# Selective scans of two hybrid layers beside piecewise side work: pieces that tell how long they hold PSUM, and a shifted order of rows, copies and stores

## The chip, the core and the metric

The kernel runs on one core of a Trainium2 chip. The metric is the device time of one execution in microseconds (us). The program is one launch that takes the whole network from its inputs in HBM to its output in HBM. The core's engines are TensorE (PE; PEld is its weight load), VectorE (DVE), ScalarE (ACT), GpSimd (POOL), and SyncE (SP), whose queue issues the DMA transfers here.

## The reference

`x` has shape (4, 64, 64, 96) in float32: four images of 64 x 64 positions with 96 channels. Layers 0 and 1 each add a gated selective scan of the group-normalized `x`; layers 2 and 3 are token-wise (linear attention and a feed-forward part whose operands are rounded to an 8-bit float format).

```
x = x + scan_layer_0(group_norm(x));  x = x + scan_layer_1(group_norm(x))
t = tokens(x)
for l in (2, 3): t = t + attention_l(ln(t));  t = t + quantized_ffn_l(ln(t))

def scan_layer(x):                                  # 192 inner channels, N = 16 states
    xi, z = split(x @ in_proj_w.T)
    xc = silu(depthwise_conv3x3(xi) + conv_b)
    for k in range(4):                              # four orders (directions) of the 4096 positions
        u = xc in order k
        dts, B, C = split(x_proj_w[k] @ u)
        dt = softplus(dt_w[k] @ dts + dt_b[k])
        h[t] = exp(dt[t] * A) * h[t-1] + dt[t] * u[t] * B[t]       # per channel and state
        y_k[t] = sum over states of h[t] * C[t]  +  D[k] * u[t]
    y = layernorm(y_0 + y_1 + y_2 + y_3, each back in the image's order)
    return (y * silu(z)) @ out_proj_w.T
```

In layer 0 the four directions are rows, columns, and both reversed. In layer 1 they are rows, and windows of 2, 4 and 8 positions.

## The kernel before

**The main loop.** Two images form a pair, and a layer of a pair is a *phase*: phases 0 and 1 are layer 0, phases 2 and 3 layer 1. Each phase has four directions k, each direction four blocks of TB = 1024 time steps. These 64 blocks are run one after the other, and a block is named phase.direction.block, counted from 0. A block has 48 *tiles*: two groups of eight state numbers n, by three thirds j of the channels, by the eight n of the group. A tile's number in its block, 0 to 47, is its *place*. A tile is 128 partitions (64 channels times two states) by 1024 steps; each n stands for two states of one image.

The loop (L1045 to L1095) runs `i` over all 3072 tiles and issues for each `i`, by hand and in this order, work of several tiles. `begin(i + 2)` (L646) makes the scan's first operand: for n in `POOL_N = (1, 4, 7, 10, 13)` a GpSimd product of du with a row of B (L652), otherwise `decays`, the ScalarE Exp (L669). `row(i + 2)` (L657) spreads the row of B over the partitions of a PSUM tile with PE (L662), for the other n. `scan(i)` (L678) is the VectorE scan (L684), followed by a ScalarE copy of the last column, the state (L690). `product(i + 1)` is the VectorE product in PSUM (L676). `weigh(i)` (L692) is the GpSimd product with a row of C (L695). `gather` (L720) folds the states of two tiles on PE into `psY` (L727). After eight tiles `flush(i - 3)` (L732) copies the sum out of `psY` on ScalarE (L739, or L743 after the second group); the second one then issues the store of `ynew` to `yd` in DRAM (L744). `resume` (L706) adds the older sum on PE (L718), and `recall(i + 7)` loads it (`yold`, L704).

**Rows.** `rows_of` (L626) lists, for every tile, the rows of C (`crep`) 7 tiles ahead and those of B (`brep`) 9 tiles ahead; `spread` (L636, L642) issues each as two broadcast DMAs from `bc` in DRAM. They share a ring of 11 buffers.

**The next block.** At place 0, `prepare` (L501) lays out, by place, what the next block needs: loads of the convolution's output (L529, `xraw` L532 for k other than 0), a permuting copy (L538), the projection on PE (L543), the copy `rows` (L549) and its store to `bc` (L555), `cut` (L559) and `take` (L564, L565) for three bf16 parts, `steps` (L569), `biased` (L576), `softplus` (L582), the input product `inputs` on GpSimd (L585), and `twice` (L587, L592), twelve copies by DMA for `deltas` and twelve for `dus`, which put one image's 64 channels on both halves of a tile. With base = 18 for k = 0 and 14 otherwise, the projection begins at place base and the softplus is at base + 15. `prepare` returns the places base - 1 to base + 14 as *kept*: in these no side work runs.

**Side work in pieces.** The convolution of a coming phase (`conv_pieces`, L212), the tail of a finished phase (`tail_pieces`, L313) and the loading of later weights (`mlp_weights`, L167) are generators, chained by `behind` (L997). Each `yield` ends a *piece*, and `advance()` runs the next piece, one at each tile outside the kept places. A piece says at its end `False`, `True` (a PSUM slot of `psM` is still in use) or `MORE` (a convolution tap follows). After `MORE` a second piece runs in the same tile if `late_by` says that the convolution is behind. At the first kept place, `while holds: advance()` runs, in that one tile, as many pieces as it takes to free the slot; at the first place with a task of the next block, pieces are forced until the convolution rows that this block reads are done. This document calls three or more pieces in one tile a *heap*. `psM`, for all side work and the next block, has 2 slots; `psB` has 2, `psY` 1.

A convolution row-pair (`t`) is: its pads, loaded in the piece before (`load` at L260, L273), normalized by ScalarE (L283); then for each j nine taps of two matmuls (L289), the SiLU `xo` (L296), two matmuls for z (L299), the SiLU `zo` (L304) and both stores (L305, L306), the last three in one piece with `xo`. A tail unit of 256 positions is: loads of `yu` and `zu` (L320, L321) and of `xr` at the unit's start, transposes (L360), statistics on ScalarE (L346 and after), the power on GpSimd (L372), normalizing (L380), transposes back (L387), scaling (L392), gates on VectorE (L398), the out-projection with its residual in two pieces, one for each image (L440 and L442, or L426 and L428 where the output is tokens), the copies `xn` on ScalarE and their stores.

On PE, DVE, ACT and POOL the instructions run in the order of the program text as the generators unroll it. SP's order is set by the framework's scheduler, so its DMAs stand in an order of their own. After the loop, `run` (L758) schedules layers 2 and 3 from lists of steps, with what is left of the last phase's tail among them.

Of the kernel before, what the change touches and what calls it, by code (L numbers as in the profile page):

```python
# [15 lines left out]
C = 96  # L16
# [6 lines left out]
T = 512  # L23
# [11 lines left out]
def kernel(ctx: ExitStack, tc: tile.TileContext, ins, out, layers=(0, 1, 2, 3)):  # L35
# [131 lines left out]
    def mlp_weights():  # L167
# [11 lines left out]
        def quantized(q, src, shape):  # L179
            t = wide(shape, "wq")  # L180
            nc.sync.dma_start(t, src)
            yield False
            yield False
            nc.vector.tensor_copy(q, t, saturate=False)
# [22 lines left out]
    MORE = 2  # L207
# [4 lines left out]
    def conv_pieces(w, xin, xc, zg, done):  # L212
# [9 lines left out]
        yield False  # L222
        yield False
        for i in range(2):
            stats = small([C, NT, 6], "gst")
            for t in range(NT):
                if t:
                    yield False
                nc.vector.bn_stats(stats[:, t, :], xbs.pop(0))
                if i * NT + t + 3 < 2 * NT:  # L230
                    xbs.append(part_of(i * NT + t + 3))
            mv = small([C, 2], "gmv")
            nc.vector.bn_aggr(mv, stats)
            yield False
            pm = psM([C, 1])
            nc.tensor.matmul(pm, gmat, mv[:, 0:1], start=True, stop=True)
            yield True
            mean = small([C, 1], "gmean")
            nc.vector.tensor_copy(mean, pm)
            dev = small([C, 1], "gdev")  # L240
            nc.vector.tensor_sub(dev, mv[:, 0:1], mean)
            nc.vector.tensor_mul(dev, dev, dev)
            nc.vector.tensor_add(dev, dev, mv[:, 1:2])
            yield False
            pv = psM([C, 1])
            nc.tensor.matmul(pv, gmat, dev, start=True, stop=True)
            yield True
            t = small([C, 1], "grs")
            nc.vector.tensor_scalar_add(t, pv, 1e-5)
            scale = small([C, 1], f"gscale{i}")  # L250
            nc.gpsimd.tensor_tensor(scale, t, mhalf[0:C, 0:1], ALU.pow)
            yield False
            shift = small([C, 1], f"gshift{i}")
            nc.vector.scalar_tensor_tensor(shift, mean, -1.0, scale, ALU.mult, ALU.mult)
            norms.append((scale, shift))
# [20 lines left out]

        done.append(now[0])
        coming = load(0)
        for t in range(NT):
            pads, coming = coming, None  # L280
            yield False
            for i in range(2):
                nc.scalar.activation(pads[i][1], pads[i][1], AF.Identity, bias=norms[i][1], scale=norms[i][0])  # L283
            yield False
            for j in range(J):
                px = psM([128, T])
                for tap in range(9):
# [6 lines left out]
                    yield MORE if tap < 8 else True  # L294
# [3 lines left out]
                for i in range(2):  # L298
# [3 lines left out]
                    )  # L302
                zo = thin([128, T], "zo")
                nc.scalar.activation(zo, pz, AF.Silu)  # L304
                nc.sync.dma_start(xc[:, j, t * T : (t + 1) * T], xo)  # L305
                nc.sync.dma_start(zg[:, j, t * T : (t + 1) * T], zo)  # L306
                if j == J - 1 and t + 1 < NT:
                    coming = load(t + 1)
                if j == J - 1:
                    done[0] += 1  # L310
                yield False

    def tail_pieces(w, units, y, zg, xin, xout, tokens):  # L313
# [10 lines left out]
        coming = None  # L324
        for t in units:
            tt = slice(t * U, (t + 1) * U)
            if coming is None:
                while t * U >= flushed(y):
                    yield False
                coming = load(t)  # L330
                yield False
                yield False
# [4 lines left out]
            xr = st([C, 2, U], F32, "xr", 1)  # L337
            for i in range(2):
                nc.sync.dma_start(xr[:, i, :], xin[i][:, tt])
# [17 lines left out]
            for q in range(2):  # L357
# [5 lines left out]
                if q:  # L363
                    statistics(0, pts)
                pts = pt
                yield True
            statistics(1, pts)
            yield False
# [5 lines left out]
            yield False  # L374
            yield False
# [25 lines left out]
            yield False  # L401
            pn0 = back(0)
            normalize(1)
            yield True
            scaled(pn0)
            pn1 = back(1)
            yield True
            scaled(pn1)
            yield True
            gate(0, pn0)  # L410
# [3 lines left out]
            yield True  # L414
            gate(1, pn1)
            yield True
            if tokens:
                xo = thin([128, 2, 2, C], "xn")
                pos = []
                for i in range(2):  # L420
# [8 lines left out]
                    yield True  # L429
                for i in range(2):  # L430
                    nc.scalar.copy(xo[:, i], pos[i][:, :, 0:C])
                    nc.sync.dma_start(xout[i][tt].rearrange("(q p) c -> p q c", p=128), xo[:, i])
                ready[0] = t + 1
            else:
                xo = thin([C, 2, U], "xn")
                pos = []
                for i in range(2):
# [5 lines left out]
                    yield True  # L443
                for i in range(2):
                    nc.scalar.copy(xo[:, i, :], pos[i])
                    nc.sync.dma_start(xout[i][:, tt], xo[:, i, :])
            yield False
# [53 lines left out]
    def prepare(ph, k, t):  # L501
# [47 lines left out]
        def rows(s):  # L549
# [4 lines left out]
            nc.scalar.copy(rests[s], pps[s])  # L554
            nc.sync.dma_start(p["bc"][:, halves[s]], rests[s][0 : 4 * N])  # L555
# [45 lines left out]
        for j in range(J):  # L601
# [10 lines left out]
            copies = max(32 + 8 * j, base + 17)  # L612
# [4 lines left out]
        for s in range(2):  # L617
            at(base + 3 + s, rows, s)
            for q in range(3):
# [6 lines left out]
    def rows_of(at, g):  # L626
# [3 lines left out]
        for n in range(g * GN, (g + 1) * GN):  # L630
            for v in (0, 1):
                if v or n in POOL_N:
                    out.append((first + n - g * GN - (7 if v else 9), at, v, n))
# [98 lines left out]
    def flush(i):  # L732
# [11 lines left out]
        nc.sync.dma_start(made[at]["img"](yd[ph][:, j, :]), yb)  # L744
# [270 lines left out]
    made, reps, sums, states, scanned, order = {}, {}, {}, {}, {}, [None]  # L1015
    end = len(tiles)
    now, rest = [0], (L - TB) // 256
    with tc.manual_schedule(engines=MANUAL):
# [9 lines left out]
        aside, holds, todo = None, False, {}  # L1028

        def advance():  # L1030
            nonlocal aside, holds
            holds = next(aside, None) if aside is not None else None
            if holds is None:
                aside = None
# [11 lines left out]
        for i in range(-9, end + 4):  # L1046
# [22 lines left out]
            if 0 <= i < end:  # L1069
# [5 lines left out]
                if plan:  # L1075
# [9 lines left out]
                    if place == kept[0]:  # L1085
                        while holds:
# [3 lines left out]
                if aside is not None and not (plan and place in kept):  # L1090
                    advance()
                    if holds == MORE and late_by(i, blocks[at][0]):
# [119 lines left out]
```

## Time and profile before

| what | value |
|---|---|
| median of three runs | 11,167.48 us (11,153.49 to 11,181.56) |
| profiled execution | 11,149.85 us |
| its span | 11,148.1 us |
| mean granted clock of TensorE | 0.87 |
| busy PE, DVE, ACT, POOL | 80%, 89%, 58%, 92% of the span |
| first scan starts, last scan ends | 134.5 us, 10,545.7 us |
| DMA | 1,604.57 MB, mean 144 GB/s |

A line of the profile's group view gives source line, engine, operation, the tile written and those read with partitions x elements and type, the number of instructions; then busy time and mean ns of one; then the idle time of the engine just before these, and which instruction ended most of it. A line of the wait view says who waited for whom: us in total, times, longest. A timeline line gives the start and the duration in us, engine, line, operation; a bracket at its end holds the idle time just before it and what ended it. "SPq" is the issue of a DMA on SP's queue: its duration there is the time that the issue took, not the transfer. A line of the windows view gives a stretch, its length, and each engine's busy time with the number of instructions, then TensorE's granted clock, the mean busy share of the DMA engines and GB/s.

### The profile page before, as it was taken

What the parts mean: (1) busy time and instruction counts of PE and PEld (TensorE: products, weight loads), DVE (VectorE), ACT (ScalarE), POOL (GpSimd) and SP (SyncE); (2) the same over time, 40 slices, a digit from 0 to 9 for tenths busy, and PEclk for the clock granted to TensorE, in tenths of its full rate; (3) what the DMA queues carried; (4) which work ended last, traced back from release to release, by engine and by line L of the source; (5) the groups of instructions that cost most, each with busy time, mean ns of one, the idle gap of its engine ahead of it and who ended that gap; (6) DMA issues with size and microseconds to landing.
All of it is one profiled execution on the core that took longest, in us unless ns stands there. A gap on an engine that the chain in (4) does not pass through costs nothing. (4 is left out here: it accounts for less than half of the span.)

```text
span 11148.1 us, 101994 instructions
## 1 busy us (share of the span) xinstructions
PE 8910.0 (80%) x30112; PEld 2880.5 (26%) x30112; DVE 9926.4 (89%) x6431; ACT 6423.1 (58%) x10575; POOL 10204.6 (92%) x5102
## 2 busy tenths in 40 slices
PE   7978888777777779887788878887778877778777
PEld 2222222111222212221222222222222322222365
DVE  3898999999999889989999999999999999999846
ACT  3656556554566646665566656665466655555576
POOL 3989999999999889999999999999999999999846
PEclk8989999888888889998888889998888888888877
DMA  5679976897578885798666656665556565556410
GB/s 134 158 141 162 141 160 157 145 134 136 149 171 151 140 151 149 157 159 132 138 169 157 157 146 169 164 159 143 149 157 156 155 149 148 143 137 159 122 33 22
DMA packets 1848188, 1604.57 MB, mean 144 GB/s; under 512 B 1412298, under 2 KB 1482892, under 8 KB 1847628
## 3 DMA queue, kind: packets, MB, share of 16 engines
q1 hardware_dynamic: 1847628, 1598.04, 66.1%
q8 instruction: 237, 3.88, 0.2%
q14 instruction: 323, 2.65, 0.1%
HBM read 1008.37 MB, written 186.65 MB: 107 GB/s over the span
## 5 line engine op out<-in xcount | busy, mean ns | idle before, releaser
L695 POOL TENSOR_TENSOR f<-f,crep 128x1024 f32<-128x1024 f32 x3072 | 7158.9, 2354 | 395.9 <-DVE f L684 296.6
L727 PE MATMUL psY<-f,fold 128*64 128x512 f32 x12288 | 3795.1, 698 | 183.4 <-POOL f L695 182.8
L684 DVE TENSOR_TENSOR_SCAN f<-f,state,psB 128x1024 f32<-128x1024 f32 x1584 | 3717.8, 2347 | 206.2 <-ACT f L669 50.1
L669 ACT ACTIVATE f<-delta,L_a 128x1024 f32<-128x1024 f32 x2112 | 2406.5, 1145 | 903.9 <-PE psY L727 829.8
L676 DVE TENSOR_TENSOR psB<-psB,du 128x1024 f32<-128x1024 f32 x2112 | 2558.9, 1212 | 362.9 <-PE psB L662 322.1
L662 PE MATMUL psB<-spB,sel 96*128 96x512 bf16 x4224 | 1387.8, 414 | 1613.5 <-DVE f L684 1599.0
L652 POOL TENSOR_TENSOR f<-du,brep 128x1024 f32<-128x1024 f32 x960 | 2265.7, 2360 | 127.2 <-PE psY L727 29.4
L684 DVE TENSOR_TENSOR_SCAN f<-psB,state,f 128x1024 f32<-128x1024 f32 x720 | 1676.7, 2329 | 76.8 <-POOL f L652 50.3
L727 PEld LDWEIGHTS psY<-f,fold 128*64 128x64 f32 x12288 | 974.9, 154 | 2525.3 <-issue 1806.8
L690 ACT COPY state<-f 128x1 f32<-128x1 f32 x2304 | 429.7, 188 | 2065.8 <-DVE f L684 2056.7
L669 ACT ACTIVATE psB<-delta,L_a 128x1024 f32<-128x1024 f32 x960 | 1070.2, 1115 | 696.0 <-DVE f L684 636.1
L684 DVE TENSOR_TENSOR_SCAN f<-f,psB 128x1024 f32<-128x1024 f32 x528 | 1208.3, 2288 | 57.6 <-ACT f L669 5.9
L662 PEld LDWEIGHTS <-sel 96*128 96x128 bf16 x4224 | 271.3, 99 | 3320.4 <-DVE f L684 2163.7
L289 PE MATMUL psM<-pad,wf 96*64 96x512 f32 x3456 | 901.4, 623 | 36.0 <-ACT pad L283 28.9
L684 DVE TENSOR_TENSOR_SCAN f<-psB,f 128x1024 f32<-128x1024 f32 x240 | 545.6, 2273 | 102.9 <-ACT psB L669 60.0
L718 PE MATMUL psY<-ysum,ident 128*128 128x512 f32 x768 | 554.5, 862 | 98.3 <-ACT ynew L743 86.7
L585 POOL TENSOR_TENSOR xs<-delta,xs 128x1024 f32<-128x1024 f32 x192 | 452.7, 2358 | 95.0 <-ACT delta L582 95.0
L569 PE MATMUL psM<-proj,dtw 12*128 12x512 f32 x768 | 455.2, 686 | 0.0
L543 PE MATMUL psM<-xs,xp 128*76 128x512 f32 x768 | 414.7, 651 | 5.5 <-DMA xs<-xcd 4.2
L718 PE MATMUL psY<-yold,ident 128*128 128x512 f32 (+2 forms) x960 | 370.6, 526 | 42.2 <-ACT ysum L739 26.7
L289 PEld LDWEIGHTS psM<-pad,wf 96*64 96x64 f32 x3456 | 221.4, 138 | 501.0 <-issue 422.6
L743 ACT COPY ynew<-psY 128x1024 f32<-128x1024 f32 (+2 forms) x312 | 242.4, 818 | 171.5 <-PE psY L727 171.5
(149 smaller groups left out, 6644.6 us busy)
## 6 DMA issues: line engine op xcount, KB each, us to landing
crep<-bc SPq DMA_DIRECT2D x2048, 256.0 KB, 4.8
delta<-delta SPq DMA_DIRECT2D x768, 256.0 KB, 4.8
du<-xs SPq DMA_DIRECT2D x768, 256.0 KB, 6.2
brep<-bc SPq DMA_DIRECT2D x640, 256.0 KB, 4.9
yd<-ynew SPq DMA_DIRECT2D x192, 512.0 KB, 7.8
xraw<-xcd SPq DMA_DIRECT2D x144, 512.0 KB, 8.5
yold<-yd SPq DMA_DIRECT2D x144, 512.0 KB, 8.9
xcd<-xo SPq DMA_DIRECT2D x96, 256.0 KB, 3.0
```

The lines of the kernel that those rows point to most:

```text
L289: nc.tensor.matmul(px[64 * i : 64 * i + 64], w["wf"][:, tap, 64 * j : 64 * j + 64], pads[i][0][:, tap // 3 : tap // 3 + rows, tap % 3 : ta ...
L569: nc.tensor.matmul(pds[-1], order[0][1][64:76, j, :], rests[s][64:76], start=True, stop=True)
L585: nc.gpsimd.tensor_mul(xs[j], deltas[j], xs[j])
L652: nc.gpsimd.tensor_mul(f[:, 1:], made[at]["dus"][j][n % 2], reps[at, 0, n])
L662: nc.tensor.matmul(scanned[i][0][:, ss], sel[:, n, :], made[at]["parts"][:, ss], start=True, stop=True)
L669: nc.scalar.activation(out, made[at]["deltas"][j][n % 2], AF.Exp, scale=W[phases[ph][0]]["a"][:, k, j, n // 2 : n // 2 + 1])
L676: nc.vector.tensor_mul(scanned[i][0], scanned[i][0], made[at]["dus"][j][n % 2])
L684: nc.vector.tensor_tensor_scan(f[:, 1:], a, bu, 0.0 if t == 0 else states[at - 1][:, c : c + 1], ALU.mult, ALU.add)
L690: nc.scalar.copy(states[at][:, c : c + 1], f[:, TB : TB + 1])
L695: nc.gpsimd.tensor_mul(f[:, 0:TB], f[:, 1:], reps[at, 1, n])
L718: nc.tensor.matmul(o, of, v, start=(m % banks == 0), stop=False)
L727: nc.tensor.matmul(py[64 * e : 64 * e + 64, ss], fold, two[e][:, ss], start=False, stop=(n == g * GN + GN - 1),)
```

## The change

Pieces now end with a tuple: `free(ahead)` says that no PSUM slot is held, and that a sequence of `ahead` pieces follows that should fit before the kept places; `held(left, more)` says that a slot is held for `left` more pieces. The loop computes the `room` left before the kept places and runs a piece after a `free` only if `ahead` fits in it; a second piece runs after a tap if the convolution is late or if `left` would otherwise not fit. The convolution and the tail are re-cut: `xo` and the z matmuls are one piece and `zo` the next, z's store and the tail's output stores are issued one or more pieces later, the next pads are loaded at the start of the last j, four tiles instead of two stand between a first load and its use, `xr` is loaded after the first normalizing, and the gates come after the next unit's loads. The store of `bc` comes two tiles after the copy `rows`, rows 5 and 7 tiles ahead instead of 7 and 9, copies at 34 + 8j instead of max(32 + 8j, base + 17), and the store of `ynew` two tiles after `flush`. Line numbers shift by up to 29 in the kernel after.

```diff
-    MORE = 2
+    def free(ahead=0):
+        return 0, ahead, False
+
+    def held(left, more=False):
+        return left, 0, more
...
         xbs = [part_of(n) for n in range(3)]
-        yield False
-        yield False
+        for _ in range(4):
+            yield free()
...
         coming = load(0)
+        yield free()
+        yield free()
         for t in range(NT):
             pads, coming = coming, None
-            yield False
...
-            yield False
+            yield free(6)
             for j in range(J):
+                if outs:
+                    outs.pop()()
+                if j == J - 1 and t + 1 < NT:
+                    coming = load(t + 1)
...
-                    yield MORE if tap < 8 else True
+                    yield held(10 - tap, tap < 8)
...
+                yield held(1)
                 zo = thin([128, T], "zo")
                 nc.scalar.activation(zo, pz, AF.Silu)
                 nc.sync.dma_start(xc[:, j, t * T : (t + 1) * T], xo)
-                nc.sync.dma_start(zg[:, j, t * T : (t + 1) * T], zo)
-                if j == J - 1 and t + 1 < NT:
-                    coming = load(t + 1)
-                if j == J - 1:
-                    done[0] += 1
-                yield False
+                outs.append(lambda j=j, t=t, zo=zo: nc.sync.dma_start(zg[:, j, t * T : (t + 1) * T], zo))
+                yield free(6 if j < J - 1 else 0)
+            outs.pop()()
+            done[0] += 1
...
                 coming = load(t)
-                yield False
-                yield False
+                for m in range(4):
+                    yield free(3 if m == 3 else 0)
...
             normalize(0)
-            yield False
+            xr = st([C, 2, U], F32, "xr", 1)
+            for i in range(2):
+                nc.sync.dma_start(xr[:, i, :], xin[i][:, tt])
+            yield free(5)
             pn0 = back(0)
             normalize(1)
-            yield True
+            yield held(4)
             scaled(pn0)
             pn1 = back(1)
-            yield True
+            yield held(3)
             scaled(pn1)
-            yield True
-            gate(0, pn0)
+            yield held(2)
             n = units.index(t) + 1
             if n < len(units) and units[n] * U < flushed(y):
                 coming = load(units[n])
-            yield True
+            yield held(1)
+            gate(0, pn0)
             gate(1, pn1)
-            yield True
+            yield free(3)
...
-                    yield True
+                    yield held(2 - i)
...
+            outs.append(away)
+            yield free(3 if coming else 0)
+            if coming is None:
+                outs.pop()()
...
-            copies = max(32 + 8 * j, base + 17)
+            copies = 34 + 8 * j
...
             at(base + 3 + s, rows, s)
+            at(base + 5 + s, spill, s)
...
-                    out.append((first + n - g * GN - (7 if v else 9), at, v, n))
+                    out.append((first + n - g * GN - (5 if v else 7), at, v, n))
...
-        nc.sync.dma_start(made[at]["img"](yd[ph][:, j, :]), yb)
+        stored[i] = made[at]["img"](yd[ph][:, j, :]), yb
+
+    def store(i):
+        if i in stored:
+            nc.sync.dma_start(*stored.pop(i))
...
-        for i in range(-9, end + 4):
+        for i in range(-9, end + 6):
+            store(i - 5)
...
                     if place == kept[0]:
-                        while holds:
+                        while holds[0]:
                             advance()
...
-                if aside is not None and not (plan and place in kept):
+                room = kept[0] - place if plan and place < kept[0] else per
+                if aside is not None and not (plan and place in kept) and (holds[0] or holds[1] <= room):
                     advance()
-                    if holds == MORE and late_by(i, blocks[at][0]):
+                    if holds[2] and (late_by(i, blocks[at][0]) or holds[0] >= room):
                         advance()
```

## The prediction

> **What bounds the kernel now.** I read the page's first part, then its costliest groups, then a table by stage, then the waits, then timelines at the longest waits. A stage is one direction of one phase (four blocks); 1.1.2 is block 2 of direction 1 of phase 1, all from 0; "place" is a tile's number in its block, 0 to 47.
>
> ```profile
> PE 8910.0 (80%) x30112; PEld 2880.5 (26%) x30112; DVE 9926.4 (89%) x6431; ACT 6423.1 (58%) x10575; POOL 10204.6 (92%) x5102
> L695 POOL TENSOR_TENSOR f<-f,crep 128x1024 f32<-128x1024 f32 x3072 | 7158.9, 2354 | 395.9 <-DVE f L684 296.6
> L676 DVE TENSOR_TENSOR psB<-psB,du 128x1024 f32<-128x1024 f32 x2112 | 2558.9, 1212 | 362.9 <-PE psB L662 322.1
> ```
>
> GpSimd is the fullest engine. A block gives it 48 weighings (L695), 15 products (L652) and 3 inputs (L585), 66 operations of about 2.35 us: 155 us. VectorE has 48 scans of about 2.33 us and 33 products of 1.21: 152 us. The shortest blocks last 153.2 us, and 64 x 153.4 = 9,818 us, while the loop's scans run from 134.5 to 10,545.7 us: 10,411. So 593 us of the loop are stalls; the change leaves the tiles' work as it is and can win only there, or in the last 602 us. By stage (us; PE, PEld, DVE, ACT, POOL busy; clock, DMA share, GB/s):
>
> ```profile
> 3431.00:4133.00 702.00, 538.09 (x1594) 162.18 (x1594) 622.59 (x376) 397.34 (x656) 622.43 (x280) 0.84 0.85 144
> 9283.00:9901.00 618.00, 462.45 (x1320) 129.87 (x1320) 591.97 (x325) 323.06 (x513) 610.66 (x265) 0.85 0.59 145
> ```
>
> These are 1.1 and 3.2: in both GpSimd works some 615 us, but 1.1 lasts 84 us longer. In the waits, VectorE's largest loss is on row matmuls that come late:
>
> ```profile
> DVE psB L676 <- PE psB L662: 322.1, 242, 13.6
> POOL f L695 <- DVE f L684: 296.6, 212, 26.1
> ```
>
> PE runs in order, and stands at something else. One case, PE then VectorE:
>
> ```profile
> 3803.71 0.61 PE L662 MATMUL psB<-spB,sel 96*128 96x512 bf16 x2
> 3816.31 2.90 PE L360 MATMUL psM<-ident,yu 128*128 128x128 f32 x12 [12.00 <-DMA yu<-yd]
> ```
> ```profile
> 3825.06 1.23 DVE L676 TENSOR_TENSOR psB<-psB,du 128x1024 f32<-128x1024 f32 x1 [13.62 <-PE psB L662]
> ```
>
> The transposes wait for yu, which the DMA queue sent only at 3810.61, because issues ahead of it took long:
>
> ```profile
> 3798.01 5.77 SPq L592 DMA_DIRECT2D delta<-delta  x1
> 3804.46 5.41 SPq L592 DMA_DIRECT2D delta<-delta  x1
> 3810.61 0.57 SPq L320 DMA_DIRECT2D yu<-yd  x1
> ```
>
> Following each VectorE gap over 1 us in the loop (206, 493 us) back to its root, I find: waits for DMA 134 (side work's own loads 68, layer 0's xraw and du copies 49, the rest phase 0.0), resume and steps matmuls 104, tail out-projections 73.5, block 0's heap 64, late GpSimd 58, convolution taps 40, tail statistics 18.
>
> **Part by part.** A tile is 153.4 / 48 = 3.19 us.
>
> *Loads of the side work.* Seven waits hold the tail or the norm: 9.0 (1.0.0), 11.8 (1.1.1), 13.6 (1.1.2), 11.7 (1.2.0), 8.7 (2.0.0), 2.8 (2.1.2), 2.0 (2.2.0), together 59.6. Four tiles instead of two after a load add 6.4 us, and a unit's loads now fall at places 32 and 46, in a block's quiet half (DMA engines idle at 26 to 29, full from 43 to about 8), with five places to the transposes: 16 us against 4.8 to 8.9 us from issue to landing. The loads at 46 meet the next burst, so not all goes: -55 (-65 to -30). Pads in 0.0, 17 us of waits, are now loaded as the last third j begins, not after its z: -5 (-17 to 0). Deferring outputs removes nothing from a bound engine: 0.
>
> *Tail out-projection.* Its two pieces fall in consecutive tiles, eight long matmuls beside a gather. PE, then VectorE:
>
> ```profile
> 6105.44 3.68 PE L727 MATMUL psY<-f,fold 128*64 128x512 f32 x8
> 6109.05 1.17 PE L440 MATMUL psM<-xr,ident 96*96 96x256 f32 x2
> 6110.15 2.87 PE L442 MATMUL psM<-zu,ow 64*96 64x256 f32 x6
> ```
> ```profile
> 6114.02 1.23 DVE L676 TENSOR_TENSOR psB<-psB,du 128x1024 f32<-128x1024 f32 x1 [5.38 <-PE psB L662]
> ```
>
> By place, pairs cost before: 3.8 us at (6,7), 10 times; 0 to 1 at (2,3), (10,11), (36,37), (40,41); 2.9 at (34,35), 2.4 at (20,21); 1.3 at (44,45); in heaps 1.7 to 13.8. They stall where the second piece comes just ahead of a GpSimd-product tile (n of 1, 4, 7, 10, 13), as such a tile gives PE 2.3 us instead of 3.5. All: 99 us (some of it counted as late GpSimd). Counting steps by the loop's rules, after has 15 pairs at place 34, 9 at 4, 15 at 0, 9 at 38, and few others: 15 x 2.5 + 9 x 3.3 + 10 = 77. So -22 (-60, if the tight places cost as little as 36; +20, if every pair at 34 and 4 costs 5). Statistics leave the heaps: -8 (-18 to 0).
>
> *Heaps.* Before, 25 tiles held three or more pieces; after, three do: block 0 (49 before, 51 after), and 0.0.1 and 0.0.2 with 23 and 24 pieces, where 13 and 5 stood, as conv work not done when the next block needs it is forced. In a heap, the tap matmuls of one third j hold PE from end to end; ScalarE's xo shows their beat:
>
> ```profile
> 198.22 0.69 ACT L296 ACTIVATE xo<-psM,L_cb 128x512 f32<-128x512 f32 x1 [3.63 <-PE psM L289]
> 207.00 0.69 ACT L296 ACTIVATE xo<-psM,L_cb 128x512 f32<-128x512 f32 x1 [7.28 <-PE psM L289]
> ```
>
> 8.8 us for one third j. Two thirds less some 6 us of cover per heap make 11.6 in each, 23 in both, against 10.8 and 1.2 before, and the spread elsewhere wins little: +15 (+5 to +35).
>
> *ScalarE.* xo and zo now stand a tile apart, with an Exp between. ACT_TABLE_LOAD goes from 303 to 461 between the two programs: 158 more.
>
> ```profile
> 1239.12 1.28 ACT L296 ACT_TABLE_LOAD   x1
> 1240.41 0.69 ACT L296 ACTIVATE xo<-psM,L_cb 128x512 f32<-128x512 f32 x1
> ```
>
> 158 x 1.283 = 203 us on an engine that is 58% full, so most lies beside GpSimd; behind a load stands the next tile's decay, which VectorE needs only two tiles later. +10 (0 to +50, a quarter uncovered). The Trainium skill ("ScalarE: Activation LUTs", section "Table sets: the hidden batching unit") speaks against this part: batch calls by table set, and a switch costs about 2.7 us with its drain. Here the row's next activation starts 1.29 us after the load's start, so no drain shows; by the page the term would be an estimated 158 x 2.7 = 427 us of ScalarE.
>
> *Rows, copies, stores.* Rows go from 7 and 9 tiles ahead to 5 and 7: 16.0 us instead of 22.3 for the crep rows, which land in 4.8 us (9.0 at most). This takes a little pressure from the 11-buffer ring. Copies move from 32, 40, 48 (35 first where k is 0) to 34, 42, 50; deltas are ready by place 29 or 33 plus the softplus, so none starts late. But the queue is one: in the issue order of layer 0's odd directions the row for place 7 moves behind yold and one xraw, the last du copy behind the third xraw. There, issues ran so:
>
> ```profile
> 1203.14 10.20 SPq L592 DMA_DIRECT2D delta<-delta  x1
> 1214.08 7.50 SPq L744 DMA_DIRECT2D yd<-ynew  x1
> ```
>
> 10.2 + 7.5 + 4.8 = 22.5 us against 16.0: 6.5 late if a row meets both, nothing if the store, now two tiles later, stays behind it. My estimate puts its landing near place 6.8 and its use at 7.7. +18 over 16 blocks (0 to +128, 8 each). The queued waiters are the later rows and copies. Layer 0's 49 us of copy stalls: 0 (-25 to +25). Resume and taps: 0 (-20 to +20). The spill two tiles later still leaves the first rows over ten tiles: 0. Final stage: 13 more tail steps land in it, 132 for 119: 0 (-8 to +8).
>
> Sum: -55 - 5 - 22 - 8 + 15 + 10 + 18 = -47. The profiled execution took 11,149.85 us (span 11,148.1), 17.6 below the median of 11,167.48; so 11,103 by the profiled run, **11,120** by the median.
>
> **Rivals.**
> (a) *A larger gain.* The pairs at 34 and 4 cost what 36 and 40 cost, 77 falls to 12, and no row is late: 11,120 - 65 - 18 = 11,037. For it: (34,35) was seen once. Against: the place is tight by its tile's kind.
> (b) *Waits only change place.* Half the load waits come back at place 46 (+30) and each tight pair costs 3.8 (24 x 3.8 + 10 = 101, +24): 11,174, no change. For it: 1.1's DMA share of 0.85. Against: five places of lead. If the heaps pay 0.87 us a piece, as block 0's 57 pieces did for 49.4 us (47 x 0.87 = 41, +14 on the forecast), the change also fails to do what it says, at 11,134.
> (c) *Slower: rows late.* In layer 0's odd directions GpSimd's weighing at place 7 waits for its row, 8 us in 16 blocks: 11,120 - 18 + 128 = 11,230. It decides from about 6.2 us a block (99 us). For it: the 10.2 and 7.5 above. Against: rows had 14 us or more before, and stores leave the way.
>
> **How the numbers follow.** A measurement of this kernel tells about 0.3%, 33.5 us, from no change: below 11,134 is faster, above 11,201 slower. Forecast, with all that ends between (a) and 11,134, 0.36; (a) 0.18; (b), to 11,201, 0.23; (c) 0.23: faster 0.54, same 0.23, slower 0.23. Taken as independent, the terms' far ends lie 58 us below and 133 above the forecast (roots of the sums of squares): 11,062 to 11,253. Stretched down to take in (a), cut a little above: 11,010 to 11,250. The faster cases alone: 11,010 to 11,134.
>
> **What would show it.** Right: 1.1 falls from 702 to below 680; yu waits under 10 us in all; VectorE's wait for row matmuls falls from 322 to about 240; pair stalls at 34 and 4. Wrong: GpSimd waits on crep rows near place 7 in 0.1, 0.3, 1.1 and 1.3 (c); table loads ahead of late decays; longer blocks 0.0.1 and 0.0.2 by over 20 us each.

## The result and the profile after

The changed kernel takes 11,363.26 us (median of 4 runs, 11,349.73 to 11,366.09), beside 11,170.94 us for the kernel before in the same comparison: a ratio of 1.0171, 95% interval 1.0154 to 1.0189. It is slower by about 192 us; the forecast was 11,120 us, and the range ended at 11,250.

The profiled execution has a span of 11,358.7 us, 210.6 more than before. The scans' loop takes 10,592.4 us instead of 10,411.1 (+181), the final stage 629.6 instead of 602.4 (+27), the start 2 more. The page, first part and groups (lines shift: L720 is the weighing, L701 the VectorE product, L709 the scan, L687 the row matmuls):

```profile
PE 8983.0 (79%) x30112; PEld 2909.1 (26%) x30112; DVE 9943.2 (88%) x6431; ACT 6638.9 (58%) x10733; POOL 10203.6 (90%) x5102
L720 POOL TENSOR_TENSOR f<-f,crep 128x1024 f32<-128x1024 f32 x3072 | 7163.0, 2354 | 508.9 <-DVE f L709 383.7
L701 DVE TENSOR_TENSOR psB<-psB,du 128x1024 f32<-128x1024 f32 x2112 | 2558.8, 1212 | 473.2 <-PE psB L687 424.0
```

GpSimd does the same work in the same time, and VectorE is busy 17 us longer; the rest of what VectorE and GpSimd lose is idle time in front of their work. ScalarE is busier by 216 us, and PE by 73 us with the same 30,112 matmuls: its mean granted clock is 0.858, against 0.870 before. In the waits of the same trace (us in total, times, longest):

```profile
DVE psB L701 <- PE psB L687: 424.0, 302, 6.5
POOL f L720 <- DVE f L709: 383.7, 271, 27.7
...
ACT xs L560 <- DMA du<-xs: 124.1, 12, 15.6
```

VectorE's wait for late row matmuls was forecast to fall from 322.1 us to 240 and has risen to 424.0, though its longest fell from 13.6 to 6.5: the few long waits on loads went, many short ones came. The third line stood at 32.7 us before. By stretch (stage 1.1, then the final stage, both of after):

```profile
3517.23:4210.47 693.24, 539.58 (x1544) 161.90 (x1544) 601.48 (x342) 402.52 (x697) 621.43 (x282) 0.84 0.86 142
10729.00:11358.70 629.70, 458.36 (x3276) 379.48 (x3274) 297.59 (x843) 428.63 (x1073) 351.16 (x755) 0.74 0.12 32
```

Stage 1.1 was to fall from 702 below 680; it reached 693. Below, a block's *excess* is its time over the mean tile times of ten undisturbed blocks of the kernel before, summed by place.

### The profile page after: what moved, and what is told of

The parts are those of the page before. It is cut to its first block, busy times and chain, and to the rows that moved or that the text cites. A ratio compares the mean times of both kernels' runs of the same rounds, so it can differ in the third digit from the quotient of the medians.

```text
span 11358.7 us, 102240 instructions
## 1 busy us (share of the span) xinstructions
PE 8983.0 (79%) x30112; PEld 2909.1 (26%) x30112; DVE 9943.2 (88%) x6431; ACT 6638.9 (58%) x10733; POOL 10203.6 (90%) x5102
## 5 line engine op out<-in xcount | busy, mean ns | idle before, releaser
L720 POOL TENSOR_TENSOR f<-f,crep 128x1024 f32<-128x1024 f32 x3072 | 7163.0, 2354 | 508.9 <-DVE f L709 383.7
L709 DVE TENSOR_TENSOR_SCAN f<-f,state,psB 128x1024 f32<-128x1024 f32 x1584 | 3718.1, 2347 | 262.1 <-ACT f L694 98.7
L701 DVE TENSOR_TENSOR psB<-psB,du 128x1024 f32<-128x1024 f32 x2112 | 2558.8, 1212 | 473.2 <-PE psB L687 424.0
L687 PE MATMUL psB<-spB,sel 96*128 96x512 bf16 x4224 | 1399.3, 418 | 1720.2 <-DVE f L709 1692.0
L709 DVE TENSOR_TENSOR_SCAN f<-psB,state,f 128x1024 f32<-128x1024 f32 x720 | 1677.0, 2329 | 110.8 <-ACT psB L694 73.9
L709 DVE TENSOR_TENSOR_SCAN f<-f,psB 128x1024 f32<-128x1024 f32 x528 | 1207.6, 2287 | 58.9 <-ACT f L694 9.3
L687 PEld LDWEIGHTS <-sel 96*128 96x128 bf16 x4224 | 274.3, 99 | 3413.7 <-DVE f L709 2205.0
L709 DVE TENSOR_TENSOR_SCAN f<-psB,f 128x1024 f32<-128x1024 f32 x240 | 545.5, 2273 | 76.6 <-ACT psB L694 46.6
```

Of the source, the lines that this page charges most:

```text
L687: nc.tensor.matmul(scanned[i][0][:, ss], sel[:, n, :], made[at]["parts"][:, ss], start=True, stop=True)
L701: nc.vector.tensor_mul(scanned[i][0], scanned[i][0], made[at]["dus"][j][n % 2])
L709: nc.vector.tensor_tensor_scan(f[:, 1:], a, bu, 0.0 if t == 0 else states[at - 1][:, c : c + 1], ALU.mult, ALU.add)
L720: nc.gpsimd.tensor_mul(f[:, 0:TB], f[:, 1:], reps[at, 1, n])
```

## The experiments

Differences in us are of medians; "before" is the run of the kernel before in the same comparison. e1 to e4, e5 to e8, e9 to e12, e13 to e15, and e16 with e17 ran together; differences across these groups carry the few us by which the kernel before differs between them (medians of 11,159 to 11,168). Excess, waits, loop and final stage come from the one profiled execution of a run, which can lie some 20 us from its median. Theory at the start: the issue order and the pieces each cost something. Rival: one of them costs all.

### Order or pieces: e1 to e4, e9

**e1**, the kernel before with the order alone:

```diff
-            copies = max(32 + 8 * j, base + 17)
+            copies = 34 + 8 * j
-                    out.append((first + n - g * GN - (7 if v else 9), at, v, n))
+                    out.append((first + n - g * GN - (5 if v else 7), at, v, n))
+            at(base + 5 + s, spill, s)
+            store(i - 5)
```

> The kernel before with only the shifts of the issue order: rows 5 and 7 tiles ahead, copies at 34 + 8j, the bc store and the ynew store two tiles later; pieces as before. Theory A (the loss is in the order: layer 0's odd directions wait about 10 us a block at places 15 and 16 for xraw and du behind later copies): +120 to +200 us over the kernel before, and about 10 us per block at those places. Theory B (the order costs only those stalls and a few late rows, the pieces cost the rest): +50 to +85 us. Theory C (order free, pieces cost all): within 20 us of the kernel before.

Measured: 11,247.82 against 11,162.58 us, ratio 1.0071 (1.0056 to 1.0086), +85. The excess at places 14 to 16 of layer 0's odd directions (1 and 3) rises from 48 to 113 us, and the final stage is 602.4 us, as before.

**e2**, the changed kernel with the lines of e1 taken back.

> The changed kernel with the old issue order (rows 7 and 9 tiles ahead, copies at max(32 + 8j, base + 17), both stores at once); pieces and pacing as changed. Theory A: within 60 us of the kernel before. Theory B: +90 to +150 us over it, with the heaps of blocks 0.0.1 and 0.0.2, the stalls at places 2, 12 and 37 and the longer blocks 1.2.0, 2.2.0 and 3.2.0 all still there, and the stalls at place 15 as in the kernel before. Theory C: +190 us.

Measured: 11,292.94 us, ratio 1.0112 (1.0097 to 1.0127), +130. Places 14 to 16 of the odd directions: 33 us. Final stage: 630.5. So both cost: theory B. The two parts make 215 us, a little more than the whole change's 192.

**e3**, the kernel before with the rows alone (the second pair of lines above).

> The kernel before with rows 5 and 7 tiles ahead and nothing else. If late rows are the price (rival c of the prediction), +80 us or more and GpSimd waits on crep rows at places 7 to 10 of layer 0's odd directions. If not, -5 to +15 us.

Measured: 11,179.22 us, ratio 1.0014 (1.0005 to 1.0024), +17. In front of the weighing GpSimd does wait for crep rows, 41.2 us in 8 waits, the longest 6.6 (2.9 us in 5 before), all at the weighing of tile 7 in blocks of layer 0's odd directions, where rival (c) put them: its mechanism exists, in 8 blocks of 16 and at an eighth of its price. The profiled execution was the fastest of the ten, 11,158.26 us, so the waits are shown, but not that they make up the 17 us.

**e4**, the kernel before with the copies alone (the first pair).

> The kernel before with copies at 34 + 8j and nothing else. If the two tiles by which copies come later are what makes the permuting copies of layer 0's odd directions late, +40 to +70 us, in places 15 and 16 of those blocks. If the order of the queue among rows, copies and stores matters and not the copies alone, within 20 us.

Measured: 11,204.79 us, ratio 1.0033 (1.0023 to 1.0043), +42; the excess at places 14 to 16 rises from 48 to 98 us.

**e9**, the kernel before with the two stores alone (the last two lines of the diff).

> The kernel before with only the ynew store and the bc store two tiles later. Theory: stores two tiles later push the sum that the next direction reads, and the rows, back in one queue: what e1 lost beyond rows (16) and copies (37), some 25 us, is theirs: +15 to +35 us. Rival: the stores are free, and the rest of e1 is rows and copies colliding in the queue: within 10 us.

Measured: 11,187.52 against 11,166.1 us, ratio 1.0015 (1.0006 to 1.0024), +21. No place stands out: VectorE gaps that go back to a DMA grow from 169 to 199 us in all, spread over xraw, the pads, brep rows and xr. Rows 17, copies 42 and stores 21 make 80 of e1's 85.

### Why later copies stall: e8, e10

In e4, ScalarE in block 0.1.2:

```profile
1255.07 1.12 ACT L669 ACTIVATE psB<-delta,L_a 128x1024 f32<-128x1024 f32 x1
1270.90 1.93 ACT L538 COPY xs<-xraw 128x1024 f32<-128x1024 f32 x1 [14.72 <-DMA du<-xs]
1272.73 1.15 ACT L669 ACTIVATE f<-delta,L_a 128x1024 f32<-128x1024 f32 x1
```

The permuting copy of the *next* block (place 13) writes into a ring of three xs buffers. It stands 14.72 us until the last du copies, which read the old contents, have landed, and the decays of the coming tiles stand behind it on ScalarE. **e8** turns the order of the last third round, in e4:

```diff
-            for m, key in enumerate(("deltas", "dus")):
+            for m, key in enumerate(("deltas", "dus") if j < J - 1 else ("dus", "deltas")):
```

> The kernel with only the copies later (e4), and for the last third j = 2 the du copies ahead of the delta copies. Theory R (recycling): the permuting copy of the next block waits for the buffer that the last du copies read; du copies four tiles earlier set it free, and the excess at places 14 to 16 of layer 0's odd directions falls from 98 us to 30 or less, the time by 50 us or more against e4. Theory L (landing): the last four copies of a block land too late for their own use at place 16, whichever they are; then the excess stays above 70 us and the wait is on delta copies instead.

Measured: 11,152.83 against 11,159.43 us, ratio 0.9997 (0.9988 to 1.0006), 52 below e4; excess 98 to 64. The same moment in e8:

```profile
1248.66 1.95 ACT L538 COPY xs<-xraw 128x1024 f32<-128x1024 f32 x1 [3.97 <-issue]
1250.51 1.16 ACT L669 ACTIVATE f<-delta,L_a 128x1024 f32<-128x1024 f32 x1
...
1259.11 1.12 ACT L669 ACTIVATE psB<-delta,L_a 128x1024 f32<-128x1024 f32 x1 [7.27 <-DMA delta<-delta]
```

The wait for the buffer is gone (in e4 it makes 78.8 us in 10 waits, in e8 none is left), and some of it comes back as a wait for delta copies, now last. Place 15 loses 62 us, place 16 gains 28: both theories hold, recycling for the larger part.

**e10** makes the same edit in the kernel before.

> The kernel before with only the du copies of j = 2 ahead of its delta copies (copies at their old places). If the permuting copies of layer 0's odd directions wait for the buffer that the last du copies read also here (48 us at places 14 to 16), some of it goes: -10 to -35 us. If the delta copies, then last, are late for place 16 in their stead, within 10 us.

Measured: 11,145.96 against 11,166.1 us, ratio 0.9984 (0.9975 to 0.9993), 20 below, as the first expectation had it. No wait of the permuting copy for the du copies is left.

### What the pieces cost: e5 to e7, e16, e17

**e5**, e2 with xo beside zo:

```diff
-                xo = thin([128, T], "xo")
-                nc.scalar.activation(xo, px, AF.Silu, bias=w["cb"][:, j, :])
                 pz = psM([128, T])
...
                 yield held(1)
+                xo = thin([128, T], "xo")
+                nc.scalar.activation(xo, px, AF.Silu, bias=w["cb"][:, j, :])
                 zo = thin([128, T], "zo")
```

> The pieces-only kernel (e2) with xo moved into zo's piece, so that the two SiLU follow each other again; as many pieces as before. Theory: the 158 added table loads crowd ScalarE at places 11 to 13, where the permuting copies and the ysum copy stand, and delay the next group's matmuls. Then table loads return to about 303 and the excess at places 11 to 13 falls by 30 to 45 us, the time by 30 to 50 us against e2. Rival: the loads lie beside other work, as the prediction had it; then within 15 us of e2.

Measured: 11,273.66 us, ratio 1.0097 (1.0079 to 1.0115), 19 below e2; table loads 299; excess at places 11 to 13 from 90 to 68 us. That lies between the two expectations: most of the 203 us of loads is hidden, about 20 us show where the loads crowd. After, block 2.2.3, ScalarE and then PE:

```profile
7385.13 1.12 ACT L560 COPY xs<-xraw 128x512 f32<-128x512 f32 x2
7386.27 1.28 ACT L307 ACT_TABLE_LOAD   x1
7387.57 0.69 ACT L307 ACTIVATE xo<-psM,L_cb 128x512 f32<-128x512 f32 x1
7388.27 1.28 ACT L694 ACT_TABLE_LOAD   x1
7389.57 1.15 ACT L694 ACTIVATE f<-delta,L_a 128x1024 f32<-128x1024 f32 x1
7390.74 1.28 ACT L316 ACT_TABLE_LOAD   x1
7392.04 0.60 ACT L316 ACTIVATE zo<-psM 128x512 f32<-128x512 f32 x1
7392.53 1.01 ACT L764 COPY ysum<-psY 128x1024 f32<-128x1024 f32 x1
```
```profile
7393.59 3.78 PE L743 MATMUL psY<-yold,ident 128*128 128x256 f32 x8 [4.10 <-ACT ysum L764]
```

The copy of ysum, which PE needs, stands behind three loads and their operations.

**e6**, e2 with an empty piece between the out-projections:

```diff
-                    yield held(2 - i)
+                    yield held(3 - 2 * i)
+                    if i == 0:
+                        yield held(2)
```

> The pieces-only kernel (e2) with one empty piece between the two out-projection pieces, so that they no longer stand in neighbouring tiles. Theory: two pieces of 4 us of PE in neighbouring tiles stall the row matmuls, about 3.4 us a pair at places 0, 4 and 34, some 110 us in all; then the excess at places 2, 7, 37 and 40 falls by 70 to 110 us and the time by 60 to 100 us against e2, less 1 to 2 tail units that move into the final stage (up to +30 us). Rival: one such piece alone is too long beside a GpSimd tile; then half of that or less.

Measured: 11,201.81 us, ratio 1.0034 (1.0023 to 1.0044), 91 below e2; excess at place 2 from 59 to 7, at 37 from 90 to 60; final stage 631.4. That seemed to settle neighbouring tiles as the cause, but the edit also moves pieces off places 0 and 35. **e16** keeps the pieces apart and the first at its old places: e6's edit, and

```diff
             nc.gpsimd.tensor_mul(nb, nmean, rstd)
             yield free()
-            yield free()
```

> The pieces-only kernel (e2) with the two out-projection pieces apart, as in e6, but with the first of them left at its places 0, 4, 34 and 38 (one empty piece before the normalizing is taken out for it). Theory N (neighbouring tiles are the price): as e6, the excess at place 2 falls from 59 to about 10 and the time by 60 to 90 us against e2. Theory S (the spot is the price: at place 0 the piece stands between two row matmuls right after PE has stood idle some 5 us, and PE's matmuls then last nearly twice as long): the excess at place 2 stays at 45 us or more, and the time falls by 20 to 45 us.

Measured: 11,285.64 against 11,168.31 us, ratio 1.0103 (1.0088 to 1.0118), 7 below e2. In the blocks with tail pieces (phases 1 to 3) the excess at place 2 is 53 us (55 in e2), as theory S has it, and at place 37 it is 44 (81). The time falls less than either theory said: against e2, stalls of 9 to 12 us each are added at places 0, 4, 36 and 38. **e17** keeps them neighbours and shifts them:

```diff
             gate(1, pn1)
+            yield free(4)
             yield free(3)
```

> The pieces-only kernel (e2) with the out-projection pieces next to each other as they were, but later: mostly at places 2 and 3, 6 and 7, 35 and 36, 39 and 40. Theory N: the stalls move along, within 25 us of e2. Theory S: the excess at place 2 falls from 59 to about 10, and the time by 30 us or more, though the pairs at 6 and 7 (3.8 us each in the kernel before) cost about what those at 4 and 5 did.

Measured: 11,225.46 us, ratio 1.0045 (1.0028 to 1.0061), 67 below e2. In the same blocks place 2 falls from 55 to under 7, place 37 from 81 to 30, place 9 rises from 7 to 40 (pairs at 6 and 7). So at place 0 neighbouring is not the price, and my theory of e6 fell; the spot is. At places 34 and 35 both edits help, and the runs do not separate the two. PE after, block 1.1.2, places 0 and 1, then VectorE:

```profile
3868.24 1.03 PE L687 MATMUL psB<-spB,sel 96*128 96x512 bf16 x2 [5.03 <-DVE f L709]
3869.07 1.06 PE L455 MATMUL psM<-xr,ident 96*96 96x256 f32 x2
3870.06 2.87 PE L457 MATMUL psM<-zu,ow 64*96 64x256 f32 x6
3872.86 3.68 PE L752 MATMUL psY<-f,fold 128*64 128x512 f32 x8
3876.47 0.84 PE L687 MATMUL psB<-spB,sel 96*128 96x512 bf16 x2
3877.15 0.59 PE L455 MATMUL psM<-xr,ident 96*96 96x256 f32 x2
3877.68 1.53 PE L457 MATMUL psM<-zu,ow 64*96 64x256 f32 x6
```
```profile
3877.35 1.23 DVE L701 TENSOR_TENSOR psB<-psB,du 128x1024 f32<-128x1024 f32 x1 [3.35 <-PE psB L687]
```

PE has stood 5.03 us waiting for a psB buffer. Then the same six matmuls take 2.87 us that take 1.53 us seven microseconds later, and the gather 3.68 us. The windows view of these two stretches shows why: TensorE's granted clock (third number from the end) is 0.50 in the first and 1.00 in the second.

```profile
3868.24:3876.47 8.23, 8.23 (x18) 2.98 (x18) 5.66 (x3) 1.41 (x3) 4.64 (x2) 0.50 1.04 231
3877.15:3882.75 5.60, 5.60 (x14) 1.76 (x12) 5.29 (x3) 4.11 (x7) 5.60 (x3) 1.00 1.59 122
```

One piece on that slow stretch makes the next row late; the second piece costs nothing. The first piece lasts 3.9 us and the second 2.1, so the clock makes, as an estimate, some 1.8 of VectorE's 3.35 us. No run puts the piece there at full clock. e17 at the same place has only the row and the gather on it:

```profile
3813.17 1.03 PE L685 MATMUL psB<-spB,sel 96*128 96x512 bf16 x2 [4.26 <-DVE f L707]
3814.14 3.68 PE L750 MATMUL psY<-f,fold 128*64 128x512 f32 x8
3817.75 0.76 PE L685 MATMUL psB<-spB,sel 96*128 96x512 bf16 x2
3818.35 0.59 PE L456 MATMUL psM<-xr,ident 96*96 96x256 f32 x2
3818.87 1.53 PE L458 MATMUL psM<-zu,ow 64*96 64x256 f32 x6
```

The Trainium skill ("TensorE: Matmul & The Clock Gate", section "What's actually happening") gives a rule for this: after an idle window of about 3.4 us the array runs at half its clock until it has been kept busy for about as long. The first half agrees with these rows (5.03 and 4.26 us of idle time, a clock of 0.50, a factor of 1.9 in the six matmuls), though in the kernel after two idle times of 1.58 and 2.56 us with one row between them were also followed by 0.50 (3996.50 to 4003.20). The second half does not agree, and the measurement decides: the clock came back after 4.6 us of unbroken PE work in e17, after 8.2 in the rows of after, and in the kernel before only after 16.7 us, at the pair that the prediction quotes:

```profile
6100.82:6117.50 16.68, 16.68 (x36) 5.78 (x36) 11.09 (x6) 5.45 (x11) 12.24 (x6) 0.50 0.80 201
6117.60:6122.00 4.40, 4.40 (x34) 3.70 (x36) 3.77 (x4) 4.23 (x13) 4.23 (x2) 1.00 0.05 17
```

By the clock at their start, 13 of the 64 out-projection pieces of phases 0 and 1 run at half clock before, 29 in the kernel after and in e2, 27 in e16, 18 in e6 and 8 in e17. The count alone does not order the times (e6 with 18 is faster than e17 with 8): where a slow piece stands counts too.

**e7**, e2 without the look-ahead in the first and last phase:

```diff
-                if aside is not None and not (plan and place in kept) and (holds[0] or holds[1] <= room):
+                if aside is not None and not (plan and place in kept) and (
+                    holds[0] or holds[1] <= room or blocks[at][0] in (0, len(phases) - 1)
+                ):
```

> The pieces-only kernel (e2) with the look-ahead of free pieces switched off in the first and the last phase. Theory: places left empty by the look-ahead are what makes the heaps of blocks 0.0.1 and 0.0.2 (32 us over the kernel before) and what pushes 13 tail steps into the final stage (28 us); then -40 to -60 us against e2, final stage about 602 us. Rival: the finer cut of the convolution and the longer tail unit do it; then within 20 us of e2 and heaps as before.

Measured: 11,274.48 us, ratio 1.0102 (1.0083 to 1.0121), 18 below e2; final stage 604.5 us, loop as in e2 (10,522.6). So the final stage's 26 us go with the look-ahead, as the theory had it. The excess of blocks 0.0.1 and 0.0.2 falls only from 67 to 57 us, and blocks 0.0.0, 0.0.3 and 0.1.1 give it back.

### Mended versions: e11 to e15

**e11**, the kernel before with e10's edit and an empty piece between the out-projections.

> The kernel before with du first for j = 2 and one empty piece between the two out-projection pieces. The pairs cost about 99 us in the kernel before; if neighbouring tiles are their whole price, -60 to -110 us against the kernel before, with up to +30 us in the final stage for tail units that are left over.

Measured: 11,190.92 against 11,166.1 us, ratio 1.0022 (1.0013 to 1.0031): the loop is 9 us shorter than before, the final stage 642.8 us, 40 longer. The 60 to 110 us did not come; 12 of the 64 pieces still start at half clock, against 13 before.

**e12**, e2 with the edits of e5, e6, e10 and, in the last phase only, e7.

> The pieces-only kernel (e2) with all remedies: xo with zo (e5, about -18), pairs apart (e6, -91), no look-ahead in the last phase (e7's final stage, -26), du first for j = 2 (-10 to -35). If the parts add up, 11,293 less 145 to 170: 11,125 to 11,150 us, at or a little below the kernel before; if they share the same slack, 11,160 to 11,190 us.

Measured: 11,166.16 us, ratio 0.9993 (0.9984 to 1.0001): loop 10,360.0, final stage 644.4. The parts do not add up; the time is that of the kernel before.

**e13**, the same, with the empty piece only before the last phase's tail:

```diff
-                    if i == 0:
+                    if i == 0 and y is not yd[-1]:
                         yield held(2)
```

> e12 with the empty piece between the out-projections only in the tails of the first three phases. e12's loop was 51 us shorter than the kernel before's and its final stage 42 us longer. Theory: one more piece in each of the nine tail units that are left costs the final stage its 42 us; then the final stage is back at 602 to 610 us, the loop gives some 5 to 15 us back in stage 3.3, and the time is 25 to 45 us below the kernel before. Rival: the pieces before the loop's end, not those in the final stage, set the tail back; then the final stage stays above 630 us.

Measured: 11,135.39 against 11,163.23 us, ratio 0.9980 (0.9971 to 0.9988): loop 10,372.2, final stage 607.4. It is 28 below the kernel before, as the theory had it. One more step in each of the last phase's tail units costs the final stage 37 us (644.4 to 607.4).

**e14**, e13 with z, xo and zo in one piece (`yield held(1)` between z and zo taken out, `held(9 - tap, ...)`).

> e13 with the z matmuls, xo and zo in one piece, 10 pieces a third instead of 11, as in the kernel before. Theory: the finer cut (two more pieces for each of the 8 row groups) is why the convolution is behind in blocks 0.0.1 and 0.0.2 and is forced there; then the heaps' excess in these two blocks (58 us in e12, 35 in the kernel before) falls to about 35 and the time by 15 to 30 us against e13. Rival: the look-ahead leaves places empty there; then within 10 us.

Measured: 11,115.42 us, ratio 0.9963 (0.9949 to 0.9977), the fastest version here and 20 below e13, as the theory had it; excess of blocks 0.0.1 and 0.0.2 from 63 to 38 us.

**e15**, e14 with the look-ahead off in the first phase too.

> e14 with the look-ahead off in the first phase as well. If the look-ahead holds a share of the heaps: another -10 to -20 us in blocks 0.0.1 and 0.0.2 against e14. If the finer cut was all of it: within 8 us of e14.

Measured: 11,134.42 us, ratio 0.9979 (0.9969 to 0.9988): the two blocks fall to 22 us, but others rise (block 0.0.0 by 14, 0.0.3 by 12 us), and the time is 19 above e14. The finer cut makes the larger part of the bigger heaps, the look-ahead a part that pays for itself elsewhere.

## Why the prediction was wrong, step by step

| step | forecast, us | measured, us | from |
|---|---|---|---|
| side work's loads and pads | -60 | -54 | VectorE gaps rooted there, 72.5 to 18.7 |
| out-projection pairs | -22 | +72 | VectorE gaps rooted there, 72 (26 gaps) to 144 (50) |
| tail statistics | -8 | not separated | |
| heaps | +15 | +29 | blocks 0.0.0 to 0.0.2 |
| table loads | +10 | +19 | e5 |
| rows | +18 | +17 | e3 |
| copies | 0 | +42 | e4 |
| stores | 0 | +21 | e9 |
| final stage | 0 | +27 | 602.4 to 629.6, e7 |

The measured column mixes medians of runs with gaps of one profiled execution, so its sum is rough. It makes +173 of the profile's +211; the rest is not located (blocks 1.2.0, 2.2.0 and 3.2.0, where the norm and the last weights now run, are 54 us longer together and hold part of it).

**Right:** The loads were right, the rows in their size, and the table loads within their bounds. The long waits for yu, pads and xr went as forecast (PE's transposes wait 9.3 us for yu in all, 32.4 before): rival (b)'s return at place 46 did not come. The rows' +17 has an interval of 6 to 27 us, so that it meets +18 so closely is luck. Rival (c) named the right side, and its late rows came at the place that it named; but they cost 17 us, not 128, and make only 14 us of waits at tile 7 in the kernel after. The rest of the loss has other causes.

**Out-projection: wrong sign.** The step that failed is "0 to 1 at (2,3)", carried over to the 15 pairs at place 0, which the sum held within the 10 us for all the rest. VectorE's gaps behind them make 50 us, 3.3 each; those behind the 15 pairs at place 34 make 54, where the sum had 37.5. I made a rule from the kind of the next tile. At place 0 the price is that PE has just been idle and the first piece runs at half clock: the trace of before shows this at the quoted pair, where 4.20 us of idle time stand ahead of the row at 6100.82 and the six matmuls take 2.87 us. I read that as "eight long matmuls", not as slow ones. Their mean says the same for the whole program:

```profile
L442 PE MATMUL psM<-zu,ow 64*96 64x256 f32 x384 | 116.4, 445 | 3.6 <-DVE zu L398 3.6
```
```profile
L457 PE MATMUL psM<-zu,ow 64*96 64x256 f32 x384 | 138.1, 510 | 0.0
```

The first line is of before, the second of after: the same 384 matmuls, placed in slower stretches (422 ns in e17).

**Copies: a missed wait.** "So none starts late" looked at what the copies need, not at who waits for them to end. Behind the last du copy stands the next block's permuting copy through a ring of three, and behind that ScalarE. The layer's 48 us of stalls at these places, whose change I held at 0 with 25 either way, were for a good part this wait already: 32.7 us in 5 waits before, 78.8 in 10 in e4, 124.1 in 12 after. Where it stood before there was no slack left, and the two tiles (6.4 us) came on top: in block 0.3.1 it grew from 7.8 to 15.4 us in e4.

**Stores: 0 was wrong.** The store of ynew had no cost in the sum, only a possible help for a late row; the store of bc had 0 because the first rows kept over ten tiles. Both looked at the store's own reader and not at what else stands in the one queue. That a deferred store takes its turn there from something that is due fits e9's larger DMA gaps (169 to 199 us), but no row shows which transfer gave way: the cost is measured, its path is not shown.

**Final stage: mis-sized.** I counted the 13 tail steps and gave them nothing; they measured 27 us, and e7, which takes the look-ahead away, gives 26 back. A unit of some 14 steps comes there about every 28 us, so by an estimate of 2 us a step 13 steps are some 27 us. That the tail's last unit sets the end is not shown: its last copy `xn` starts 264 us after the last scan before and 278 after, only 14 later, and at 275 in e7, whose final stage is 604.5.

**Heaps: mis-sized.** Two thirds per heap less 6 us of cover were 11.6; measured gaps are 20.5 and 19.0 us. The path back from these gaps runs over the decays, ScalarE's pads and zo, and PE's taps without a break: nothing covered them. The 0.87 us a piece that rival (b) took from block 0 came closer: 47 pieces make 41 us by it, and the two gaps are 39.5.

## What to carry over

Before costing a transfer that is moved later, list who waits for its end: the reader of its target, and whoever reuses its source. Before giving a matmul a price by its kind, look at the idle time ahead of it and at the granted clock: the same six matmuls took 1.53 or 2.87 us here. Count added steps of paced work as time where little else is left to run beside it: 13 steps went with 27 us of the final stage here, and one more step in each unit with 37.

## What the runs showed of the hardware

VectorE instructions of 96 x 1 elements took up to 4.59 us. After, block 2.2.0, VectorE and then GpSimd:

```profile
6984.40 0.14 DVE L254 TENSOR_SCALAR grs<-psM 96x1 f32<-96x1 f32 x1
...
6988.78 4.59 DVE L259 SCALAR_TENSOR_TENSOR gshift<-gmean,gscale 96x1 f32<-96x1 f32 x1 [0.77 <-POOL gscale L256]
```
```profile
6988.72 2.35 POOL L677 TENSOR_TENSOR f<-du,brep 128x1024 f32<-128x1024 f32 x1
6991.02 2.33 POOL L720 TENSOR_TENSOR f<-f,crep 128x1024 f32<-128x1024 f32 x1
```

It lasts from just after the start of one GpSimd product to the end of the next. The same line took 0.15 us in the first norm, where GpSimd has nothing to do, and the neighbour that reads PSUM takes 0.14. The Trainium skill ("SBUF — State Buffer", section "Who interferes with whom") states that a VectorE instruction with two inputs in SBUF contends with a GpSimd instruction that reads SBUF; these rows agree. In the kernel before this line takes up to 3.0 us.
